# Row maxima of the softmax: turned by VectorE in blocks of 32 and carried through DRAM, in place of four products with the identity

## The chip, the core and the metric

The kernel runs on one core of a Trainium2 chip. Its time is that of one execution in device microseconds. Before the change the median of three runs was 5038.61 us (5038.29 to 5046.06).

The core has five engines that run side by side, each through its own instructions in order: TensorE (PE in the profile; its weight loads are PEld), VectorE (DVE), ScalarE (ACT), GpSimd (POOL) and SyncE (SP). SP issues nearly all the transfers (DMAs) of this kernel, one after the other. Engines wait for each other through semaphores.

## The reference

One transformer block on `x` of shape 4 x 2048 x 512 in float32: a normalization, then attention with 16 heads of 32 columns and a mixture of two experts per sequence, both added to `x`.

```python
x = L0_attn_x
xn = _layernorm(x, axis=-1)
x = x + _L0_attn_ref(xn, ...) + _L0_ffn_ref(xn, ...)

qkv = jnp.einsum('bnc,dc->bnd', x, qkv_w) + qkv_b
attn = jnp.einsum('bhqd,bhkd->bhqk', q, k) * scale
attn = jax.nn.softmax(attn, axis=-1)
out = jnp.einsum('bhqk,bhkd->bhqd', attn, v)

_, idx = jax.lax.top_k(x[:, 0, :] @ Wr + br, 2)
h = jax.nn.gelu(jnp.einsum('bsd,bkde->bkse', x, W1[idx]) + b1g, approximate=False)
o = jnp.einsum('bkse,bkef->bksf', h, W2[idx]) + b2g
```

The softmax needs, for every query and head, the largest score over its 2048 keys. The change concerns how these maxima get from where they are computed to where they are subtracted.

## The kernel before

**Units and chunks.** Attention is cut into chunks of 512 queries for one sequence (4), one group of four heads (4) and one quarter of the queries (4): 64 chunks. A chunk is worked in 16 units, one for each tile of 128 keys, so there are 1024 units, about 4.9 us each (the span over their number). The main loop `for U in range(-LEAD, plan.units)` issues one unit per turn, for all engines; the order is written out by hand (`manual_schedule`), and each engine keeps the order in which the loop names its work.

**Two passes.** Every unit does two things. The first pass (`score_max`, L715) makes scores with queries in the partitions, for a chunk that is 22 units ahead (`LEAD` = 16 + 6); VectorE takes the negated maximum of each 128x512 tile (L855) into `mx`. The second pass makes the scores again with keys in the partitions: `shift` (L725) first writes minus the row maximum into the four banks of the unit, as a product of ones (`ones_b`) with `negm`, and `score` (L733) adds the scores. ScalarE takes the exponential (L849), `weigh` (L745) multiplies with the values in every second unit, GpSimd sums the weights (L766). Besides that a unit holds at most one dense item (`dense`, L485) that a plan puts there: a piece of the projections or of the experts.

**The way of the maxima.** In the last unit of a chunk's first pass, call it unit 0, `split` reduces `mx` to 16 numbers for each query row (4 heads x 4 query tiles, L794). GpSimd's part of it (`rest`, L799 and L801) is issued in unit 1: it splits each number into three bfloat16 parts whose sum is the float32 number, and lays them in three of every 32 columns of `spread`, all other columns being zero. In unit 4 `turn_maxima` transposes `spread` with four products with the identity (L809), and VectorE copies the result from PSUM to `negm` (L812): head j then has its parts in partitions 32 j to 32 j + 2, and queries along the free axis. The first `shift` that reads it stands at the head of unit 7.

**SP's queue.** `later(u, f)` runs f at the end of unit u; stores of results are put off by two or three units this way. Loads are issued at the end of the unit in which their buffer is free and no earlier than eight units before their use (`Plan.loads`). SP goes through all of these in the order of issue and waits at each one for what it needs: for a store that the data is there, for a load that the buffer is no longer read. Each DMA also takes one of eight completion semaphores in turn, and may be issued when the DMA eight places before it has landed.

Of the kernel before, what the change touches and what calls it, by code (L numbers as in the profile page):

```python
# [9 lines left out]
F32 = mybir.dt.float32  # L10
BF16 = mybir.dt.bfloat16
U32 = mybir.dt.uint32
AF = mybir.ActivationFunctionType
ALU = mybir.AluOpType
AX = mybir.AxisListType
SP = mybir.EngineType.SP

P = 128
HEADS = 16
HD = 32  # L20
GH = P // HD
TOP_K = 2
EPS = 1e-5
CH = 512
# [214 lines left out]
def block_kernel(  # L239
# [16 lines left out]
    nc = tc.nc  # L256
# [3 lines left out]
    NT = N // P  # L260
    NCH = N // CH
    TPC = CH // P
    SCALE = float(HD) ** -0.5
    PSUM = bass.MemoryType.PSUM
    plan = Plan(B, DC, NCH, NT, TPC)
# [3 lines left out]
    const = ctx.enter_context(tc.tile_pool(name="const", bufs=1))  # L269
# [4 lines left out]
    small = ctx.enter_context(tc.tile_pool(name="small", bufs=2))  # L274
    ps = ctx.enter_context(tc.tile_pool(name="ps", bufs=8, space=PSUM))

    def bank(name):
        return ps.tile([P, CH], F32, tag="bank", name=name)
# [6 lines left out]
    for b in range(B):  # L285
        for k in range(TOP_K):
            ws_dram[b, k] = tc.dram_tile([P, DC, D], F32, name=f"ws_dram_{b}_{k}")
    wqk_dram = [tc.dram_tile([P, DC, D], F32, name=f"wqk_dram_{n}") for n in range(2)]
    for b in range(B):
        for c in range(NCH):  # L290
# [90 lines left out]

    ident = const.tile([P, P], F32, name="ident")
    make_identity(nc, ident)
    ident_b = const.tile([P, P], BF16, name="ident_b")
    nc.vector.tensor_copy(ident_b, ident)
    ones = const.tile([P, HD], F32, name="ones")
    nc.gpsimd.memset(ones, 1.0)
    ones_b = const.tile([P, P], BF16, name="ones_b")
    nc.gpsimd.memset(ones_b, 1.0)


    spread = []
    for i in range(2):
        t = const.tile([P, TPC, GH, HD], BF16, name=f"spread{i}")
        nc.gpsimd.memset(t, 0.0)
        spread.append(t)

    first = pair.tile([B, D], F32, tag="att", name="first")
    nc.sync.dma_start(first, x[:, 0, :])
# [12 lines left out]
    for n in range(2):  # L412
        wkq.append(stream.tile([P, DC, D], F32, tag="h", name=f"wkq_{n}", bufs=2))
        src = qkv_wT.rearrange("(c p) n -> p c n", p=P)[:, :, (1 - n) * D : (2 - n) * D]
# [5 lines left out]
    for n in range(2):  # L420
        src = qkv_wT.rearrange("(c p) n -> p c n", p=P)[:, :, (1 - n) * D : (2 - n) * D]
# [41 lines left out]
    pt = bank("first_ps")  # L463
# [231 lines left out]
    def place(u):  # L695
        rest, kt = divmod(u, NT)
        rest, qc = divmod(rest, NCH)
        return (*divmod(rest, DC), qc, kt)

    mx, negm, sacc, psums, sums, pT = {}, {}, {}, {}, {}, {}  # L700
    curves, waiting, ends = {}, {}, []

    def later(u, do):
        waiting.setdefault(u, []).append(do)
# [85 lines left out]

    def split(where, n):

        neg = small.tile([P, GH, TPC], F32, tag="neg", name="neg_%d_%d_%d" % where)
        nc.vector.tensor_reduce(neg, mx[where], AX.X, ALU.min)  # L794

        def rest():
            s = spread[n % 2].rearrange("p i j d -> p j i d")
            for part in range(3):
                nc.gpsimd.tensor_copy(s[:, :, :, part], neg)  # L799
                if part < 2:  # L800
                    nc.gpsimd.tensor_tensor(neg, neg, s[:, :, :, part], ALU.subtract)  # L801

        return rest

    def turn_maxima(where, n):
        negm[where] = small.tile([P, CH], BF16, tag="negm", name="negm_%d_%d_%d" % where)
        pt = ps.tile([P, CH], BF16, tag="bank", name="mt_%d_%d_%d" % where)
        for i in range(TPC):
            nc.tensor.transpose(  # L809
                pt[:, ts(i, P)], spread[n % 2][:, i].rearrange("p j d -> p (j d)"), ident_b  # L810
            )
        nc.vector.tensor_copy(negm[where], pt)  # L812

    att = {}

# [13 lines left out]
    for U in range(-LEAD, plan.units):  # L829
# [26 lines left out]
        last = U + LEAD  # L856
        if first_pass is not None and last % NT == NT - 1:
            where, n = place(last)[:3], last // NT
            rest = split(where, n)
            mark = U  # L860
            pending = (rest, where, n, mark)
        if last % NT == 0 and 0 < last <= plan.units:
            pending[0]()
        before = place(U - NT)[:3] if U >= NT else None
# [1 line left out]
        part = (kt - keys - 1) // 2 if keys == 4 else (kt - keys - 2) // 2  # L866
# [28 lines left out]
        for step, sb, n in plan.extra.get(U, []):  # L895
# [10 lines left out]
            else:  # L906
                c, i = divmod(n, TPC)
                xs = stage[sb, c] = held["xq", ("stage", sb, c)]
                turn(xs, held["xl", ("normal", sb, c)][:, i, :], i, f"{sb}_{n}")
                if i == TPC - 1:  # L910
                    later(U + 1, lambda sb=sb, c=c, xs=xs: nc.sync.dma_start(xn_dram[sb, c], xs))
        if last % NT == 3 and NT < last <= plan.units + 3:
            turn_maxima(*pending[1:3])
        for item in plan.items.get(U, []):
            dense(item, U, curve is not None, invert if two else lambda: None)

# [3 lines left out]
        for s, tag, key in loads.get(U, []):  # L920
            t = load(tag, key)
# [7 lines left out]
        for n, c in ((16, NCH - 1), (1, NCH - 2)):  # L929
            if U == plan.units - n:  # L930
                tags = ("xq", "xq") if c == NCH - 1 else ("xl", "h")
                t, rows = (
                    stream.tile([P, TPC, D], F32, tag=tag, name=f"end_{c}_{n}",
                                bufs=BUFS.get(tag, 2))
                    for n, tag in enumerate(tags)
                )
                for i in range(TPC):
                    nc.sync.dma_start(rows[:, i, :], part_dram[B - 1, c, i])
                n = DC - 1 if c == NCH - 1 else DC
# [4 lines left out]
    U = plan.units  # L944
    weigh(U - 2)
    add_last(U - 2)
    where = place(U - 1)[:3]
# [15 lines left out]
    for i in range(TPC):  # L963
        q = ts(i, P)
# [52 lines left out]
```

## Time and profile before

| | us |
|---|---|
| median of three runs | 5038.61 |
| the profiled execution, its own time | 5042.55 |
| its span, first to last instruction | 5040.8 |
| busy: PE | 4947.0 |
| busy: POOL | 4429.2 |
| busy: DVE | 3740.2 |
| busy: ACT | 2394.0 |
| mean granted TensorE clock | 0.997 |

The profile comes from one execution. A group of instructions is a line of the kernel with its engine, its operation and its operands (out<-in). The timeline gives start and duration of each instruction in us from the span's start, merging neighbours of the same kind ("x4"), and in brackets the idle time of the engine just before, with what ended it. For SP the duration is that of issuing a DMA; the time to landing is listed apart, as a median for each kind.

### The profile page before, as it was taken

Reading aid. Unit: us, or ns where it says so; the run is one execution under the profiler, and the core shown is the slowest. Engines: PE = TensorE matmul, PEld = TensorE weight load, DVE = VectorE, ACT = ScalarE, POOL = GpSimd, SP = SyncE. Lnnn points to the kernel's source line nnn. Section 1 sums busy time; section 2 is a strip of 40 time slices with the busy share of each in tenths; the row PEclk is TensorE's granted clock in tenths of the full one; section 3 lists DMA queues with packets and bytes.
Section 4 is the critical chain, followed back from the end, with each engine's and each line's share of the span. In section 5 each row is a group of like instructions: output and inputs, shape, how many; then the busy total and the mean of one; then the engine's idle time right before and its main releaser. Section 6 shows DMA issues by size and latency. Waiting matters only on the chain. (4 is left out here: it accounts for less than half of the span.)

```text
span 5040.8 us, 107883 instructions
## 1 busy us (share of the span) xinstructions
PE 4947.0 (98%) x45028; PEld 1725.8 (34%) x45028; DVE 3740.2 (74%) x5909; ACT 2394.0 (47%) x4406; POOL 4429.2 (88%) x1498
## 2 busy tenths in 40 slices
PE   8999999999999999999999999999999999999998
PEld 2333333333333333333333333333333333333332
DVE  5777887777777788777777777877777777777762
ACT  1445445454444545454444444555444445454453
POOL 2799998999898998999889998999988988999981
PEclk9999999999999999999999999999999999999999
DMA  6333334433233434434224234434423343323312
GB/s 219 111 103 117 115 96 127 142 122 109 80 107 104 126 107 122 140 114 141 89 86 125 85 121 118 146 122 136 134 70 106 100 123 101 101 80 101 107 62 95
DMA packets 297128, 568.16 MB, mean 113 GB/s; under 512 B 24636, under 2 KB 144188, under 8 KB 279744
## 3 DMA queue, kind: packets, MB, share of 16 engines
q1 hardware_dynamic: 287568, 495.19, 29.4%
q0 software_dynamic: 9072, 66.06, 6.7%
q8 instruction: 354, 5.80, 0.5%
q14 instruction: 134, 1.10, 0.1%
HBM read 367.44 MB, written 127.66 MB: 98 GB/s over the span
## 5 line engine op out<-in xcount | busy, mean ns | idle before, releaser
L766 POOL TENSOR_TENSOR psum<-psum,p 128x2048 f32<-128x2048 f32 x819 | 3722.4, 4545 | 167.6 <-ACT p L849 129.2
L849 ACT ACTIVATE p<-s 128x512 f32<-128x512 f32 x4096 | 2118.0, 603 | 2364.9 <-PE m L715 2181.8
L855 DVE TENSOR_REDUCE mx<-m 128x1 f32<-128x512 f32 x4096 | 2544.2, 684 | 570.1 <-PE m L715 569.8
L733 PE MATMUL s<-qT,kT 32*128 32x512 f32 x8192 | 1919.1, 588 | 0.0
L715 PE MATMUL m<-kT,qT 32*128 32x512 f32 x8192 | 1911.3, 590 | 6.4 <-ACT h L524 3.4
L715 PEld LDWEIGHTS m<-kT,qT 32*128 32x128 f32 x8192 | 920.9, 184 | 334.9 <-issue 244.7
L745 PE MATMUL acc<-p,v 128*32 128x512 f32 x8192 | 988.5, 600 | 37.0 <-ACT p L849 37.0
L733 PEld LDWEIGHTS s<-qT,kT 32*128 32x128 f32 x8192 | 768.6, 185 | 29.2 <-issue 7.3
L485 PE MATMUL ops<-wb_w,h 128*32 128x512 f32 x4096 | 466.0, 595 | 0.6 <-ACT p L849 0.2
L745 PEld LDWEIGHTS acc<-p,v 128*32 128x32 f32 x8192 | 214.2, 109 | 737.0 <-ACT p L849 420.5
L762 POOL TENSOR_TENSOR psum<-p,p 128x2048 f32<-128x2048 f32 x63 | 287.5, 4563 | 203.2 <-ACT p L849 203.2
L754 DVE TENSOR_TENSOR sacc<-acc,sacc 128x512 f32<-128x512 f32 x448 | 309.9, 692 | 158.3 <-PE acc L745 158.3
L485 PE MATMUL hps<-xt,wt_w 128*32 128x512 f32 x3584 | 411.0, 596 | 2.5 <-ACT p L849 2.0
L725 PE MATMUL s<-negm,ones_b 32*128 32x512 bf16 x4096 | 405.7, 385 | 6.2 <-ACT p L849 5.9
L485 PE MATMUL qkps<-xt,wt_qk 128*32 128x512 f32 x3360 | 387.8, 599 | 9.8 <-ACT p L849 9.2
L725 PEld LDWEIGHTS <-ones_b 32*128 32x128 bf16 x4096 | 103.2, 91 | 858.2 <-issue 858.1
L870 DVE RECIPROCAL sums<-sums 128x128 f32<-128x128 f32 x252 | 237.6, 943 | 0.7 <-ACT sums L784 0.7
L485 PEld LDWEIGHTS ops<-wb_w,h 128*32 128x32 f32 x4096 | 120.0, 109 | 308.6 <-issue 229.8
L633 DVE SCALAR_TENSOR_TENSOR row<-ops,row 128x512 f32<-128x512 f32 x128 | 88.4, 691 | 170.3 <-PE ops L485 116.3
L485 PE MATMUL prps<-wb_proj,xl_at 128*32 128x512 f32 x1792 | 203.9, 595 | 0.3
L485 PEld LDWEIGHTS hps<-xt,wt_w 128*32 128x32 f32 x3584 | 103.3, 109 | 268.2 <-issue 186.1
L485 PEld LDWEIGHTS qkps<-xt,wt_qk 128*32 128x32 f32 x3360 | 97.3, 110 | 273.9 <-issue 181.6
(123 smaller groups left out, 1981.6 us busy)
## 6 DMA issues: line engine op xcount, KB each, us to landing
xt<-t_dram SPq DMA_DIRECT2D x181, 512.0 KB, 4.3
xt<-xn_dram SPq DMA_DIRECT2D x133, 512.0 KB, 5.0
psum<-p POOLq DMA_DIRECT2D x63, 1024.0 KB, 8.2
part_dram<-row SPq DMA_DIRECT2D x128, 256.0 KB, 2.0
v_dram<-v SPq DMA_DIRECT2D x64, 256.0 KB, 2.7
wt_w<-ws_dram SPq DMA_DIRECT2D x128, 128.0 KB, 3.3
v<-v_dram SPq DMA_DIRECT2D x64, 256.0 KB, 4.9
row<-in_x_dram SPq DMA_DIRECT2D x64, 256.0 KB, 6.5
```

The source lines that it names most:

```text
L485: nc.tensor.matmul(pp[rows_of(j), :], lhsT[:, rows_of(j)], rhs, start=(first and n == 0), stop=(last and n == len(terms) - 1),)
L633: nc.vector.scalar_tensor_tensor(row, pp, 0.5, row, ALU.mult, ALU.add)
L715: nc.tensor.matmul(t, qT[b, g, qc][r, ts(i, P)], kT[b, g, kc][r, :], start=True, stop=True)
L725: nc.tensor.matmul(tiles[j], ones_b[r, :], negm[b, g, qc][r, :], start=True, stop=False)
L733: nc.tensor.matmul(tiles[j], kT[b, g, kt // TPC][r, ts(kt % TPC, P)], qT[b, g, qc][r, :], start=False, stop=True,)
L745: nc.tensor.matmul(acc[r, :], held["v", (b, g, kt // TPC)][:, (kt + n) % TPC, r], pT[u + n][:, j, :], start=(n == 0), stop=(n == 1),)
L754: nc.vector.tensor_tensor(t, acc, t, ALU.add)
L762: nc.gpsimd.tensor_tensor(psums[b, g, qc], pT[u - 1], pT[u], ALU.add)
L766: nc.gpsimd.tensor_tensor(psums[b, g, qc], psums[b, g, qc], pT[u], ALU.add)
L849: nc.scalar.activation(pT[U][:, j, :], tiles[j], AF.Exp, scale=SCALE)
L855: nc.vector.tensor_reduce(dst, t, AX.X, ALU.max, negate=True)
L870: nc.vector.reciprocal(sums[before][:, q], sums[before][:, q])
```

## The change

`split` now writes its 16 numbers into the first 16 of 32 columns of `negs` (the others are zero), and VectorE turns that 128x32 tile in blocks of 32x32. After it, partition 32 t + r holds the number r (head and query tile) of the queries 32 t to 32 t + 31. GpSimd splits these into the three bfloat16 parts in place of the strided `spread`. At the end of unit 3 SP stores the parts to DRAM (128 rows of 96 numbers), and at the end of unit 5 it fetches them back with 16 DMAs, one for each head and query tile: each reads 12 runs of 32 numbers and writes three partitions of `negms`. `negms` are two constant tiles, zeroed once; their other partitions stay zero. The four products with the identity, their bank in PSUM and the copy to `negm` are gone.

```diff
+    parts_dram = [tc.dram_tile([P, 3, HD], BF16, name=f"parts_dram_{n}") for n in range(2)]
...
-    ident_b = const.tile([P, P], BF16, name="ident_b")
-    nc.vector.tensor_copy(ident_b, ident)
...
-    spread = []
+    negs = []
+    negms = []
     for i in range(2):
-        t = const.tile([P, TPC, GH, HD], BF16, name=f"spread{i}")
+        t = const.tile([P, HD], F32, name=f"negs{i}")
         nc.gpsimd.memset(t, 0.0)
-        spread.append(t)
+        negs.append(t)
+        t = const.tile([P, CH], BF16, name=f"negms{i}")
+        nc.gpsimd.memset(t, 0.0)
+        negms.append(t)
...
     def split(where, n):
-        neg = small.tile([P, GH, TPC], F32, tag="neg", name="neg_%d_%d_%d" % where)
-        nc.vector.tensor_reduce(neg, mx[where], AX.X, ALU.min)
+        neg = negs[n % 2]
+        nc.vector.tensor_reduce(
+            neg[:, : GH * TPC].rearrange("p (j i) -> p j i", j=GH), mx[where], AX.X, ALU.min
+        )
+        turned = small.tile([P, HD], F32, tag="turned", name="turned_%d_%d_%d" % where)
+        nc.vector.transpose(turned, neg)
+        parts = small.tile([P, 3, HD], BF16, tag="parts", name="parts_%d_%d_%d" % where)
+        negm[where] = negms[n % 2]
 
         def rest():
-            s = spread[n % 2].rearrange("p i j d -> p j i d")
             for part in range(3):
-                nc.gpsimd.tensor_copy(s[:, :, :, part], neg)
+                nc.gpsimd.tensor_copy(parts[:, part], turned)
                 if part < 2:
-                    nc.gpsimd.tensor_tensor(neg, neg, s[:, :, :, part], ALU.subtract)
-
-        return rest
-
-    def turn_maxima(where, n):
-        negm[where] = small.tile([P, CH], BF16, tag="negm", name="negm_%d_%d_%d" % where)
-        pt = ps.tile([P, CH], BF16, tag="bank", name="mt_%d_%d_%d" % where)
-        for i in range(TPC):
-            nc.tensor.transpose(
-                pt[:, ts(i, P)], spread[n % 2][:, i].rearrange("p j d -> p (j d)"), ident_b
-            )
-        nc.vector.tensor_copy(negm[where], pt)
+                    nc.gpsimd.tensor_tensor(turned, turned, parts[:, part], ALU.subtract)
+
+        def store():
+            nc.sync.dma_start(parts_dram[n % 2], parts)
+
+        def fetch():
+            src = parts_dram[n % 2].rearrange("(t r) s q -> r s t q", t=P // HD)
+            for j in range(GH):
+                for i in range(TPC):
+                    nc.sync.dma_start(
+                        negms[n % 2][j * HD : j * HD + 3, ts(i, P)].rearrange(
+                            "s (t q) -> s t q", q=HD
+                        ),
+                        src[j * TPC + i],
+                    )
+
+        return rest, store, fetch
...
-            rest = split(where, n)
-            mark = U
-            pending = (rest, where, n, mark)
+            pending = split(where, n)
+            later(U + 3, pending[1])
+            later(U + 5, pending[2])
...
-        if last % NT == 3 and NT < last <= plan.units + 3:
-            turn_maxima(*pending[1:3])
```

## The prediction

> **What bounds the kernel.** I read the busy times first, then the group that the change removes, then SP's timeline just ahead of the chunks' first shifts, because that is where the new transfers must fit.
>
> The first and third lines of the page:
>
> ```profile
> span 5040.8 us, 107883 instructions
> ...
> PE 4947.0 (98%) x45028; PEld 1725.8 (34%) x45028; DVE 3740.2 (74%) x5909; ACT 2394.0 (47%) x4406; POOL 4429.2 (88%) x1498
> ```
>
> PE is busy all the time, so what is taken from PE is gained in full, and what makes PE wait is lost in full. The group that goes, by its tile `mt`:
>
> ```profile
> L809 PE MATMUL mt<-ident_b,spread x256: 219/219/230, 140.7 to 4913.7; 128*128 128x128 bf16 x128
> L812 DVE COPY negm<-mt x64: 360/415/416, 143.1 to 4914.0; 128x512 bf16<-128x512 bf16 x64
> ```
>
> Of the columns count, shortest/median/longest in ns, the 219 ns are no price, since products overlap. PE's timeline of one chunk (its first shift is at 1519.16) gives it:
>
> ```profile
> 1505.12 0.59 PE L733 MATMUL s<-qT,kT 32*128 32x512 f32 x2
> 1505.64 0.40 PE L809 MATMUL mt<-ident_b,spread 128*128 128x128 bf16 x4
> 1506.07 3.64 PE L485 MATMUL qkps<-xt,wt_qk 128*32 128x512 f32 x32
> ...
> 1519.16 0.40 PE L725 MATMUL s<-negm,ones_b 32*128 32x512 bf16 x4
> ```
>
> From the last score to the next product is 0.52 us in a unit without turn (1515.07 to 1515.59), and here too up to the turn. The turn adds 1506.07 - 1505.64 = 0.43 us. SP in the same chunk:
>
> ```profile
> 1508.06 0.32 SPq L319 DMA_DIRECT2D xt<-t_dram  x1
> 1509.77 0.32 SPq L319 DMA_DIRECT2D xt<-xn_dram  x1
> 1510.19 0.38 SPq L878 DMA_DIRECT2D att_dram<-att  x1
> ```
>
> In the order of the built program the 16 fetches stand between the second and the third of these. SP had waited there for PE to release the buffers of `xt`; it is free for the fetches at 1510.09, and PE wants their data at 1519.16: 9.1 us.
>
> **Taken from PE: the turns.** 64 x 0.43 = 27.5 us gained. None of them waits for anything longer than this, so there is no more to gain.
>
> **Added to SP's queue: a store and 16 fetches for each chunk.** I took this room, from SP being free before the fetches to the first shift, for all 64 chunks. There are three groups: 3 chunks with 2.5 to 3.0 us, 23 with 7.3 to 9.1 us (mean 8.5), 38 with 12 us or more. The worst is of this kind:
>
> ```profile
> 974.27 0.34 SPq L634 DMA_DIRECT2D part_dram<-row  x1
> 990.41 0.39 SPq L365 DMA_DIRECT2D xl_normal<-in_x_dram  x1
> 990.90 0.46 SPq L878 DMA_DIRECT2D att_dram<-att  x1
> ```
>
> A load of 1 MB waits for its buffer until 990.41, the fetches stand behind it, and the shift is at 993.84.
>
> How long 16 small DMAs take is not in the trace. Nearest are the only two DMAs with four partitions, at the start, among others issued back to back:
>
> ```profile
> 0.74 0.39 SPq L399 DMA_DIRECT2D first<-in_x_dram  x1
> 1.19 0.41 SPq L403 DMA_DIRECT2D x<-in_x_dram  x1
> ...
> 2.19 0.40 SPq L407 DMA_DIRECT2D br_sb<-in_br_dram  x1
> 2.63 0.35 SPq L409 DMA_DIRECT2D bqkv<-in_qkv_bT_dram  x1
> ```
>
> Start to start that is 0.45 and 0.44 us; I take 0.45. The bounds are 0.36, the least of any DMA in the trace (a 0.32 us issue and 0.04 to the next), and 0.57, that of `v<-v_dram` (0.53 and 0.04), the slowest to issue of the frequent kinds. For the landing:
>
> ```profile
> xt<-xn_dram SPq DMA_DIRECT2D x133, 512.0 KB, 5.0
> part_dram<-row SPq DMA_DIRECT2D x128, 256.0 KB, 2.0
> ```
>
> I take 2.0 us, with 1.6 below (VectorE starts on `first` 1.60 us after its issue) and 2.4 above (the median of `wt_w<-in_W_dram`). The size does not matter: the trace's packets under 64 B take 9 ns each, and a fetch has 12 of 64 B.
>
> With the queue clear a fetch takes 15 x 0.45 + 2.0 = 8.75 us. In most of the 23 chunks a 512 KB load stands just ahead, which lands 4.3 to 5 us after its issue, and the seventh or eighth fetch needs its semaphore: it goes out about 1.4 us later than its turn, and the rest follow. That makes 10.2 us. PE must wait for all of them, as the built order has four landings ahead of each of the four weight loads of the first shift. Stall: 23 x (10.2 - 8.5) = 39 us. In the three others the fetches are again behind large loads: 10 less 2.7, some 7 to 9 each, taken one by one 25 us. Sum 64 us. By the lower bounds (0.36, 1.6) the same count gives 37 us, by the upper ones (0.57, 2.4) 105 us. The 38 chunks have room at all of these.
>
> **What a long stall does to the clock.** PE sat idle three times for 3 us or more in the middle of this run, and this is the first:
>
> ```profile
> 767.43 1.21 PE L715 MATMUL m<-kT,qT 32*128 32x512 f32 x1 [3.45 <-ACT h L524]
> ...
> 764.00:776.00 12.00, 8.57 (x46) 2.39 (x50) 7.36 (x10) 5.43 (x10) 7.59 (x4) 0.72 0.69 178
> ```
>
> The second line is a stretch of 12 us; its third figure from the end is the granted clock: 0.72, that is half speed for 6.8 us. Waits of 2.47 and 2.07 us elsewhere left it at 1.00. The Trainium skill, page "TensorE: Matmul & The Clock Gate", Part 1, says that the clock falls to half after about one idle window of 3.4 us. Taken as a threshold it adds nothing in the 22 stalls below that and half of 3.4 to 6.8 us in the four above (the three, and one of the 23 with 4.3 us): 7 to 14, I take 10 us. The trace agrees on both sides, but half speed also followed a wait of only 1.46 us at 3204 us. If every stall did that, it would be 26 x 1.7 = 44 us, and that is in the upper end of the range.
>
> **Added to PE: the waits themselves.** Each of the four weight loads now has four or five semaphores to wait for, where it had one; the trace shows such an extra wait on PE as an instruction of 51 ns that takes up to two of them. Two per load hold the four loads, which start together today, 0.1 us apart: 0 to 0.4 us per chunk, as the scores of the first heads may fill the steps. I take 0.2 us where PE does not stand still anyway, 38 x 0.2 = 8 us; at most 64 x 0.4 = 26 us.
>
> **At no cost.** VectorE loses the copy (0.40 us) and gains a turn of 128x32, between the 0.22 us of the reduction beside it and 0.40: less than nothing to 0.2 us per chunk, in the 0.54 us that it waits for PE before the next unit's maxima. GpSimd's five small operations get 32 columns for 16: by the rows of 16 (230 ns) and 512 columns (1309 ns) that is 2.2 ns a column, 0.18 us a chunk, 11 us in all, hidden by its 610 us of idle time; it would be 11 us if GpSimd were the bound. `rest` keeps its place, and nothing new waits behind it. The store stands at unit 3, and the parts are ready 16 to 28 us before the shift; SP comes to it no earlier in nearly all chunks, and its 2.0 us lie ahead of the fetches. What is queued behind the fetches (at 1510.19 a store, at 1517.57 the next `xt`, held by PE anyway) is delayed by up to 8 us, but the loads that this hits have that much to spare: the thinnest is a `prow` with 4 us left. Freeing a PSUM bank changes which bank follows which, and no unit without a turn waits for that. The first instructions lose a cast and trade memsets, under 1 us.
>
> **The sum.** -27.5 + 64 + 10 + 8 = +54.5 us against the profiled time of 5042.55, 5097. That execution was 4 us above the median of its three runs, so the forecast is 5038.6 + 54.5 = 5093 us, slower by 1.1%. By the lower bounds of all terms it is -27.5 + 37 + 5 + 0 = +15, 5053; by the upper ones -27.5 + 105 + 44 + 26 = +147, 5186. I take 5050 to 5160 as this case's own range.
>
> **Rivals.** (1) The fetches fit. If the room is as I read it and the fetches end within 7.5 us even behind an `xt`, only the three chunks stall, for about 5 us each. That speaks from the 1.6 us of `first`, and from SP, which does little else. Then -27.5 + 15 + 0 is -12 us, 5026; with no stall at all 5011. It decides from a total stall of about 20 us downwards. Against it: the semaphore of a load that lands after 5 us leaves no way to have all 16 landed in 7.5. (2) The fetches take much longer, since each has DRAM as its source just after the store and goes to three partitions only: at 0.7 us a DMA the same count gives 142 us, the second row's stalls pass 3.4 us, and with 25 stalls at half clock the end is near 5200. For it is that no DMA of this shape is in the trace; against it that issues stretch beyond 0.6 us only behind several large loads. (3) The stalls are mostly hidden and the waits eat the rest: within 0.2%.
>
> **How the numbers follow.** The likeliest case 0.67, the first rival 0.12, the third 0.07, the second 0.14. A change under 0.2% can't be told from none here. So faster 0.12, same 0.07, slower 0.81. The range takes in part of the first and of the second rival: 5022 to 5170.
>
> **What would show it.** PE's rows L809 gone; SP with 17 more DMAs a chunk, 0.45 us apart; waits of PE on the weight load of the shift for the landing of `negms`, some 26 of them, mostly 1 to 2 us, three of 7 to 9 us with a dip of the clock behind; L766 and L855 unchanged. I am wrong if waits show in chunks with wide room (each fetch costs more), or in none (they are cheaper), or if the first shifts spread by more than 0.4 us.

## The result and the profile after

The changed kernel takes 5055.53 us (median of 8 runs, 5053.21 to 5059.39), the kernel before in the same comparison 5039.62: ratio 1.0028, 95% interval 1.0018 to 1.0039. It is slower by 16 us; the forecast was 54 us, so the sign was right and the size was not. The profiled execution's span is 5054.2 us, 13.4 more than before (the profiled execution of the kernel before was 3 us above its median). The page of the changed kernel, its first line, its busy times, and the groups of the shift's products and weight loads (after the bar busy time, mean ns, idle time ahead of them and what ended it):

```profile
span 5054.2 us, 109023 instructions
...
PE 4941.2 (98%) x44772; PEld 1717.7 (34%) x44772; DVE 3731.1 (74%) x5908; ACT 2394.7 (47%) x4406; POOL 4426.3 (88%) x1500
...
L729 PE MATMUL s<-negms,ones_b 32*128 32x512 bf16 x4096 | 413.7, 385 | 27.9 <-DMA negms<-parts_dram 22.2
...
L729 PEld LDWEIGHTS <-ones_b 32*128 32x128 bf16 x4096 | 104.8, 91 | 887.2 <-issue 863.7
```

PE is busy for 6 us less and its span is 13 us longer: it waits more. The list of waits has it (total us, times, longest), two rows that before had no counterpart:

```profile
PE s L729 <- DMA negms<-parts_dram: 22.2, 18, 5.5
...
PEld L729 <- DMA negms<-parts_dram: 19.1, 13, 4.0
```

Both rows describe the same standstills, once by the product and once by its weight load, so they are not added. To see what PE loses I took the start of the fourth shift of each unit in both traces, and summed by place in the chunk the difference of the intervals between them (unit numbers as above: the maxima are ready in unit 0, the first shift that reads them heads unit 7; what lies before the fourth shift of the first chunk counts with the ends):

| interval | after less before, us |
|---|---|
| unit 4, which had the turns | -26.8 |
| unit 6, with the wait at the first shift | +28.4 |
| unit 7, the first with the new maxima | +6.5 |
| unit 1 | +1.5 |
| units 9 and 10 (second pass, units 2 and 3) | +2.1 |
| all others, with the ends | +1.7 |
| sum: the span | +13.4 |

Of the +28.4, three chunks (11, 27 and 43, counted from 0) have 9.8, 6.5 and 6.6. The first of these on PE's timeline of the changed kernel:

```profile
991.33 3.64 PE L489 MATMUL ops<-wb_w,h 128*32 128x512 f32 x32
997.29 0.37 PE L729 MATMUL s<-negms,ones_b 32*128 32x512 bf16 x1 [2.32 <-DMA negms<-parts_dram]
998.03 0.37 PE L729 MATMUL s<-negms,ones_b 32*128 32x512 bf16 x1 [0.36 <-DMA negms<-parts_dram]
1003.92 0.58 PE L729 MATMUL s<-negms,ones_b 32*128 32x512 bf16 x1 [5.52 <-DMA negms<-parts_dram]
1004.74 0.58 PE L729 MATMUL s<-negms,ones_b 32*128 32x512 bf16 x1 [0.24 <-DMA negms<-parts_dram]
```

Head after head waits for its own four fetches. SP's timeline says why they are late:

```profile
991.47 0.39 SPq L366 DMA_DIRECT2D xl_normal<-in_x_dram  x1
991.91 10.65 SPq L820 DMA_DIRECT2D negms<-parts_dram  x16
```

The 16 fetches stand behind a load of 1 MB that PE had held until 991.47. It costs them twice. SP stops at the eighth, whose completion semaphore is the load's, until the load has landed:

```profile
SPq L820 <- DMA xl_normal<-in_x_dram: 2.5, 1, 2.5
```

And the four fetches of the first head, all issued by 993.3, are there only when its shift starts at 997.29, just after the load. In stretches around it the granted clock (third figure from the end) falls:

```profile
990.00:997.00 7.00, 4.97 (x44) 1.36 (x36) 3.77 (x6) 2.07 (x4) 6.63 (x3) 1.00 0.47 151
997.00:1004.00 7.00, 0.82 (x3) 0.28 (x3) 0.00 (x0) 0.00 (x0) 0.36 (x1) 0.65 0.81 169
1004.00:1010.00 6.00, 5.76 (x30) 2.27 (x33) 2.48 (x4) 2.17 (x4) 0.00 (x0) 0.56 1.03 360
```

The chunk that the forecast read line by line is the counterpart: it has one of the 23 middling rooms, and PE waits for nothing. SP and then PE there:

```profile
1525.00 0.32 SPq L320 DMA_DIRECT2D xt<-xn_dram  x1
1525.37 7.41 SPq L820 DMA_DIRECT2D negms<-parts_dram  x16
```

```profile
1530.81 3.64 PE L489 MATMUL qkps<-xt,wt_qk 128*32 128x512 f32 x32
1534.38 0.40 PE L729 MATMUL s<-negms,ones_b 32*128 32x512 bf16 x4
```

The room is 9.0 us from the first fetch to the shift, as read before, but the 16 are issued in 7.4 us and the data are there in time. SP stops in them once, for 2.0 us, at the eighth, until the `xt` in front has landed. The row of such waits over the whole run:

```profile
SPq L820 <- DMA xt<-xn_dram: 31.7, 16, 2.6
```

### The profile page after: what moved, and what is told of

Its sections match the earlier page's. It is cut to its first block, busy times and chain, and to the rows that moved or that the text cites. A ratio compares the mean times of both kernels' runs of the same rounds, so it can differ in the third digit from the quotient of the medians.

```text
span 5054.2 us, 109023 instructions
## 1 busy us (share of the span) xinstructions
PE 4941.2 (98%) x44772; PEld 1717.7 (34%) x44772; DVE 3731.1 (74%) x5908; ACT 2394.7 (47%) x4406; POOL 4426.3 (88%) x1500
## 5 line engine op out<-in xcount | busy, mean ns | idle before, releaser
L729 PE MATMUL s<-negms,ones_b 32*128 32x512 bf16 x4096 | 413.7, 385 | 27.9 <-DMA negms<-parts_dram 22.2
```

The source lines that it names most:

```text
L729: nc.tensor.matmul(tiles[j], ones_b[r, :], negm[b, g, qc][r, :], start=True, stop=False)
```

## The experiments

Ratios are those to the kernel before in the same comparison, with their intervals. In the three comparisons the kernel before took 5042.5, 5040.0 and 5040.0 us.

**The fetch one unit earlier.**

```diff
-            later(U + 5, pending[2])
+            later(U + 4, pending[2])
```

> All 64 fetches at the end of unit 4 in place of unit 5, so that they stand in SP's queue ahead of the loads that PE holds back. Theory A (the whole loss is PE standing at the first shift of a chunk, in the chunks where SP is free late; with 0.32 us a DMA and 1.55 us to land, the room is 12 us or more everywhere): no waits for negms, about 5012 us, 27 us under the kernel before. Theory B (the added transfers cost by their mere number, by delaying other loads on SP's queue and the rings): the 17 DMAs are all still there, so a good part of the 43 us between 5055 and 5012 stays, 5030 or more.

Measured: 5023.74 us, ratio 0.9961 (0.9947 to 0.9974): one number is changed, and it is faster than both kernels. The waits of PE for `negms` are gone. In chunk 11 SP now has:

```profile
970.41 5.05 SPq L820 DMA_DIRECT2D negms<-parts_dram  x16
...
987.39 0.41 SPq L366 DMA_DIRECT2D xl_normal<-in_x_dram  x1
```

With the queue clear the 16 fetches take 5.05 us, 17 us ahead of the load that had held them. Theory B, the mere number of transfers, is out as the main cause: all 17 per chunk are still there. But 5012 was expected and 5024 came, so theory A lacks something.

**Three chunks only.**

```diff
-            later(U + 5, pending[2])
+            later(U + (4 if n in (11, 27, 43) else 5), pending[2])
```

> Only the fetches of chunks 11, 27 and 43 are moved to the end of unit 4, ahead of the 1 MB load of xl_normal; the other 61 stay in unit 5. Theory A with the unit times of the two traces (these three chunks' last and first units are 12.0, 8.4 and 8.9 us longer than before): 5055 - 29 = about 5026 us, and the clock's dips at 999, 2218 and 3450 us gone. Theory B (spread over all chunks): 5053 or more, as 3 of 64 chunks are touched.

Measured: 5031.92 us, ratio 0.9981 (0.9975 to 0.9988), which is 23.6 us below the changed kernel where 29 were expected. In its trace units 6 and 7 are 30.4 us shorter than in that of the changed kernel, and units 9 and 10, with the wait of the next run, are 3.7 us longer. Three of 64 chunks turn the change from a loss to a gain. The dips of the clock at 999, 2218 and 3450 us are gone.

**No transfers at all.**

```diff
-            later(U + 3, pending[1])
-            later(U + 5, pending[2])
...
-                nc.scalar.activation(pT[U][:, j, :], tiles[j], AF.Exp, scale=SCALE)
+                nc.scalar.activation(pT[U][:, j, :], tiles[j], AF.Exp, scale=SCALE / 8)
```

> Store and fetches left out; the shift reads the zeroed tiles, and the exponent's scale is an eighth, so that nothing overflows without the maxima: the softmax is not the reference's. PE has neither turns nor waits. Theory A: 5012 us, the gain of the turns alone (64 x 0.43 = 27.5 us). If taking the turns out gives less (what follows a turn was held by something else): 5020 to 5040.

Measured: 5023.53 us, ratio 0.9962 (0.9949 to 0.9976). This is as fast as the fetch at unit 4, so those transfers cost nothing that can be measured; and it is 19 us below the kernel before, not 27. In its trace the turn's interval is shorter by 26.8 us, as in all these kernels; but units 2 and 3 of the second pass are 7.3 us longer (10.7 with the fetch at unit 4). Their size differs from trace to trace: the one with the fetch at unit 4 is of an execution 7 us above its median. There ScalarE waits for a DMA. The row of waits for it in the kernel before, then without transfers, then with the fetch at unit 4:

```profile
ACT p L849 <- DMA psum<-p: 36.3, 9, 7.4
```

```profile
ACT p L864 <- DMA psum<-p: 34.3, 7, 8.1
```

```profile
ACT p L864 <- DMA psum<-p: 51.0, 12, 8.1
```

It is the DMA by which GpSimd adds the weights of a chunk's last key tile to their sum (8.2 us to land). It holds one of four buffers of weights, and unit 3 of the next chunk needs that buffer. The total of this row does not measure what PE loses: without transfers it is no longer than before. In single chunks it can be seen. More than half of the 7.3 us, 4.1, is in chunk 13, where ScalarE's wait grows from 2.9 to 5.3 us and that of PE behind it from 0.97 to 3.38. What this DMA is worth in time is measured below, by leaving it out.

**The transfers there, but nobody waits for them.**

```diff
+    still = const.tile([P, CH], BF16, name="still")
+    nc.gpsimd.memset(still, 0.0)
...
-                tiles[j], ones_b[r, :], negm[b, g, qc][r, :], start=True, stop=False
+                tiles[j], ones_b[r, :], still[r, :], start=True, stop=False
...
-                nc.scalar.activation(pT[U][:, j, :], tiles[j], AF.Exp, scale=SCALE)
+                nc.scalar.activation(pT[U][:, j, :], tiles[j], AF.Exp, scale=SCALE / 8)
```

> Store and fetches stay as in the changed kernel, but the shift reads a third tile that is always zero, with the exponent's scale an eighth as in the run without transfers: the softmax is not the reference's. The traffic is there, nobody waits for it. Theory A: 5012 to 5015 us, as without transfers. Theory B: the traffic's own cost shows here, 5030 to 5055 us.

Measured: 5031.42 us, ratio 0.9977 (0.9967 to 0.9987), within what theory B expected. The two intervals overlap, but each of its nine executions (5026.07 us and more) took longer than each of the five without transfers (5025.71 at most). So the traffic at unit 5 costs about 8 us even where nobody waits for it. In the two traces 7.2 of their 7.4 us lie in one place, units 2 and 3 of the second pass of chunk 43. PE there without transfers, and then with them:

```profile
3436.17 0.66 PE L459 MATMUL xt<-ident,xl_normal 128*128 128x128 f32 x4 [1.16 <-ACT p L864]
```

```profile
3440.98 1.12 PE L461 MATMUL xt<-ident,xl_normal 128*128 128x128 f32 x4 [5.79 <-ACT p L866]
```

The DMA `psum<-p` that ScalarE waits for is issued at 3428 us in both and lands after 12.0 us in place of 7.8. The loads that SP issues behind the 16 fetches (two of `wt_w` and one of `xt`) go out 7 to 8 us later than without them, at 3426 to 3429, and so fall together with it. That fits, but it is one chunk of one execution each, and no run tests it.

**A fetch as long as forecast.** The fetch at unit 5 with its first six DMAs issued twice.

```diff
-            for j in range(GH):
-                for i in range(TPC):
...
+            for r in [*range(6), *range(GH * TPC)]:
+                j, i = divmod(r, TPC)
```

> The fetch at unit 5 made as long as the forecast had it: the first six DMAs are issued twice, 22 in all at the measured 0.32 us is 7.0 us of issue. Theory A (the 23 chunks of middling room were spared because a fetch takes 0.32 us on SP and not 0.45): the forecast's own count over the 64 chunks, with 0.32 us and 1.55 us to land, gives 76 us of stalls in 27 chunks for 22 fetches and 29 us for 16, so 47 us and some clock more than the changed kernel: about 5105 us. Theory D (they were spared because the load ahead holds nothing up, whatever the pitch): only the three late chunks grow by 2 us each, 5062 us.

Measured: 5107.24 us, ratio 1.0133 (1.0118 to 1.0149). Theory D is out. By place in the chunk, unit 6 is now 79.2 us longer than before (76 counted) and unit 7 is 18.3 longer; most of the middling chunks stand still for 1 to 3 us, 42.6 us in all. The three late chunks have the other 36.6, 14 more than with 16 fetches. So the forecast's count over the rooms of the middling chunks was good, and what it was fed was not: with 22 DMAs at 0.32 us, which is the length I had assumed for 16, the stalls I had forecast for them (39 us) appear. Its waits for `negms`:

```profile
PE s L729 <- DMA negms<-parts_dram: 60.4, 46, 7.3
PEld L729 <- DMA negms<-parts_dram: 44.7, 30, 8.2
```

**Four fetches in place of 16, at unit 5.** Another layout in DRAM.

```diff
-    parts_dram = [tc.dram_tile([P, 3, HD], BF16, name=f"parts_dram_{n}") for n in range(2)]
+    parts_dram = [tc.dram_tile([HD // 2, 3, CH // GH], BF16, name=f"parts_dram_{n}") for n in range(2)]
...
-            nc.sync.dma_start(parts_dram[n % 2], parts)
+            for t in range(P // HD):
+                nc.sync.dma_start(
+                    parts_dram[n % 2][:, :, ts(t, HD)], parts[t * HD : t * HD + GH * TPC]
+                )
...
+            for j in range(GH):
+                nc.sync.dma_start(
+                    negms[n % 2][j * HD : j * HD + 3, :].rearrange("s (i x) -> s i x", i=TPC),
+                    parts_dram[n % 2][ts(j, TPC)].rearrange("i s x -> s i x"),
+                )
```

> The parts are stored with four DMAs (16 rows of each block of 32) so that the fetch at unit 5 needs four DMAs, one for each head, in place of 16. Theory A: 3 x 0.32 + 1.55 = 2.5 us from SP being free to the last landing, which is within the room of every chunk (2.5 us at least): no stalls to speak of, though nothing is moved ahead in the queue; as with the fetch at unit 4, about 5023 us. Theory B (place in the queue behind the held load is what counts): the three chunks still stall for several us, 5035 or more.

Measured: 5034.3 us, ratio 0.9989 (0.9982 to 0.9995). The middling chunks have no waits left, but the three late ones still have. Chunk 43, SP and then PE:

```profile
3422.43 0.39 SPq L366 DMA_DIRECT2D xl_normal<-in_x_dram  x1
3422.87 0.51 SPq L377 DMA_DIRECT2D row<-in_x_dram  x1
3423.55 1.63 SPq L821 DMA_DIRECT2D negms<-parts_dram  x4
```

```profile
3428.29 1.00 PE L729 MATMUL s<-negms,ones_b 32*128 32x512 bf16 x4 [2.35 <-DMA negms<-parts_dram]
```

The four fetches are issued by 3425.2, and the first shift starts three us later. From the start of the last issue to the fourth shift it is 4.0 to 4.3 us in the three chunks; with 16 fetches and no 1 MB load in front it is 1.3 to 1.7 us (these fetches are four times as large, and without such a load nobody waits for them, so their own landing is not measured). So theory B holds for these three: being behind 1 MB costs beyond the time on SP, as the first head of chunk 11 above also shows. Fewer DMAs mend the length, the place mends both.

**The kernel before, and the fetch at unit 4, both without the adding DMA.**

```diff
-            nc.gpsimd.dma_start(psums[b, g, qc], pT[u], accum_op=ALU.add)
+            return
```

> The kernel before, without the DMA on GpSimd's queue that adds the weights of a chunk's last key tile to their sum (so one key tile of 16 is missing from the softmax's sums). Theory C (the turns' gain of 27 us shrinks to 19 in the runs without stalls because units 2 and 3 of a chunk wait in some chunks for this DMA to free a buffer of weights): the waits for it, 36 us, are gone; 5005 to 5020 us. Its use is as the base for the next run.

> The changed kernel with the fetch at unit 4, also without that adding DMA (one key tile of 16 missing from the softmax's sums). Theory C: against the kernel before without the DMA it is now the full 27 us faster. If the missing 8 us are lost in something else (the added transfers, the wait on 16 landings): it is 19 us or less.

Measured: 5015.46 us for the kernel before (0.9953, 0.9940 to 0.9967), 4992.40 for the changed one with the fetch at unit 4 (0.9907, 0.9891 to 0.9922). Between them are 23.1 us, where with the DMA it was 18.7. Without it units 2 and 3 of the second pass differ by 1.2 us in place of 10.7 (2.4 in the trace of the next run, which also fetches at unit 4), so the wait is named, though its size differs between executions; of the 27 us, 1.6 more go in unit 1, and the rest in small amounts. In time, 4 of the missing 8 us are shown; the intervals of the two ratios are too wide to say more.

**Both edits.** Four stores and four fetches as above, with `later(U + 4, pending[2])`.

> Both edits at once: four stores and four fetches, and the fetch at the end of unit 4. Theory A: no fetch is late after the move alone, so fewer transfers bring nothing more: the same as the fetch at unit 4, ratio 0.996 to the kernel before, about 5021 us. If the number of transfers costs beside the stalls (9 us, seven or eight fewer DMAs for each chunk): 5012 to 5015 us.

Measured: 5021.12 us, ratio 0.9966 (0.9952 to 0.9979). This can't be told from the move alone: once no fetch is late, fewer of them bring nothing that can be measured.

## Why the prediction was wrong in its size

- **The turns, -27.5.** Right where they stood: -26.8 by the trace. Wrong in "gained in full": without any stall only 19 of it reaches the end. Of the 8 us that are missing, 4 are shown to be spent waiting for the adding DMA; the rest is in part the 1.5 us of unit 1 and otherwise open. The row for that wait was in the trace of before (36.3 us) and has no place in the forecast. In the changed kernel itself this hardly shows (+2.1): chunks 38 and 43, which stall at their first shift, are 2.4 and 2.1 us shorter in these units. With 22 fetches it is even turned round, -7.3 us.
- **One fetch DMA on SP, 0.45 us.** This is the step that failed. It measured 0.32 from start to start (0.276 to issue), below my lower bound of 0.36 too. That bound was no bound: it was the quickest of the large transfers, and the two small ones that I took as nearest stood at the very start of the program. Whether their place or their shape made them slower is not shown. With the landing below it made of 5.5 us in the middling chunks a stall of 39.
- **Landing, 2.0 us.** In the chunks where PE waited, the fourth shift came 1.3 to 1.7 us after the start of the last issue, but 2.7 us in chunk 11. The lower bound of 1.6 was about right.
- **The 23 middling chunks, 39 us.** With 0.32 and 1.55 us the same count gives 8 us (29 in all, less 21 for the three); the trace has 28.4 less 22.9, so 5.5 us in unit 6. The load ahead was read rightly: in the chunk read line by line the eighth fetch goes out 4.3 us after the first, where the forecast has about 4.6 (7 x 0.45 + 1.4). What follows it was forecast at 8 x 0.45 + 2.0 = 5.6 us and by the measured times is 8 x 0.32 + 1.55 = 4.1. Of these 1.5 us, which are most of the stall of 10.2 - 8.5, about 1.0 are the issue and 0.45 the landing. The run with 22 fetches confirms the count.
- **The three late chunks, 25 us.** 22.9 us, and by the run that moves only them, 23.6 us in time with the clock. Right for the reason given: they are behind a load that PE holds. The size is in part luck: from the first fetch to the fourth shift the three took 12.8, 8.8 and 9.0 us, where each was given 10.
- **The clock, 10 us.** Three new dips, behind these three stalls; unit 7 is 6.5 us longer. Taking the idle window of 3.4 us (the Trainium skill, page "TensorE: Matmul & The Clock Gate", Part 1) as a threshold was the better of the two readings: the middling stalls of this trace, up to 2.0 us, left the clock alone. It is no sharp threshold, though. Two more dips, of 3.4 us each, are in this trace and not in that of before. That at 1177 us follows a wait of 4.24 us (0.97 before) for the adding DMA's buffer in chunk 13; that at 1999 us follows one of 1.49 us, which was 1.48 before and left the clock alone. With both edits a wait of 2.97 us (1156 us) left it alone too. And with 22 fetches, standstills of 2.5 to 4.0 us in pieces of about 1 us, head after head, were followed by a dip in six chunks and by none in three.
- **Four or five semaphores for each weight load, 8 us.** Nothing: in chunks without a wait all four shifts start within 0.01 us, as before.
- **At no cost.** GpSimd's operations take 211 and 245 ns at 32 columns (254 and 230 at 16). VectorE's turn takes 211 ns, but in unit 1 PE loses 1.5 us in all. The trace has PE's weight loads of the first pass wait for `turned` in 16 places, 3.7 us in all, while nothing had waited for the copy that went.

The measured sum is -26.8 + 28.4 + 6.5 + 1.5 + 2.1 + 1.7 = +13.4 us. The forecast's with its two times of a fetch corrected and the semaphores at nothing, -27.5 + 29 + 10 + 0, would have been +11.5. That this comes so near is in part luck: it has 3.5 us too much for the clock and lacks the last three terms, 5.3 us together.

## What to carry to other kernels

A transfer that replaces work on the bounding engine is paid for by its place in the issuing queue: here 61 of 64 chunks were nearly free and three behind a held load took the whole gain (22.9 us and 6.5 of clock against 26.8), so look for the load in front that waits for the very engine that will wait for you, and issue ahead of it. Where many small DMAs must land in a fixed room, their cost each on the queue is the number that decides; if the trace has no such DMA, a range that spans the sign is the honest forecast. Before counting time taken from the bounding engine as gained, list the waits for transfers that already end on it, since an engine that comes earlier may only wait longer there: here 8 of 27 us did not reach the end, and 4 of them are shown to be such a wait.

## What the runs showed of the hardware that was not expected

A DMA of 12 runs of 64 B goes out every 0.32 us from SP, quicker than any larger one in this kernel (0.36), and with a clear queue 16 of them are issued in 5.05 us. Right behind a load of 1 MB (chunk 11) the same 16 took 10.65 us to issue, and four larger ones needed 4.0 to 4.3 us from the start of the last issue to the fourth shift, where 16 without such a load needed 1.3 to 1.7. Waiting for 16 landings through four weight loads cost PE nothing measurable. The clock fell to half after some PE waits of 1.5 us and stayed full after one of 2.97 us.
